# Two cross-attention layers on one core: a pair's image tokens in a shared tile, packed third blocks, merged text keys, and a Gram matrix from high halves

## The chip, the cores and the metric

The kernel runs on one core of a Trainium2 chip. The metric is the device time of one execution in microseconds (us), the median of the runs. Engines in the profile: PE is TensorE's matmul, PEld its weight load, DVE is VectorE, ACT is ScalarE, POOL is GpSimd, and SP is the queue that issues most DMAs.

## The reference

Two layers run one after the other on `x` (16 batches, 256 queries, 320 channels) with a context of 16 batches, 256 tokens, 512 channels. There are 20 heads of 16 channels.

```python
# layer 0 (the first): 77 text tokens, 179 image ("ip") tokens
q, k_t, v_t = x @ Wq, text @ Wk, text @ Wv            # split into heads
text_out = softmax(q k_t / 4) v_t                     # per head
k_ip, v_ip = ip @ Wk_ip, ip @ Wv_ip
text_probs = softmax(q . k_text / 4)                  # all channels at once, no heads
sem  = (text_probs @ text) @ ip.T / 4                 # 256 x 179 per batch
ip_probs = softmax(q k_ip / 4 + 0.5 * sem) * mask
x = (text_out + ip_probs v_ip) @ Wout + bout + x
# layer 1 (the second): 252 text tokens, 4 image tokens
probs = softmax(q k_t / 4);  text_out = probs v_t     # per head
qsem  = l2norm(probs @ text)                          # per head, 512 wide
sem   = qsem @ l2norm(ip).T
ip_probs = softmax(q k_ip / 4 + 0.5 * sem) * mask
out = (text_out + ip_probs v_ip) @ W_out + b_out + x
```

## The kernel before

**Halves.** Every matmul operand that must be precise is kept as a high half (rounded to fp32r) and a low half (the remainder). A product of two such operands takes three matmuls for each 128 rows of the contraction: high x high, high x low, low x high (`prod`, L320 to L327). A product over 512 context channels is thus 12 matmuls. `halves` (L240) makes the two: ACT casts the high half, DVE or POOL subtracts.

**Layer 0** works in slots k = 0 to 79, one for each batch and group of four heads, so ten slots for a pair of batches. In a slot (`slot0`, L911) PE does the scores of slot k+2 (`score0`, tile S, 8 matmuls), the transposed scores of slot k (`turned0`, tile T, 8 matmuls), and the product with the values of slot k-1 (`attend0`, tile P). Between them lie ACT's exponentials (L899), POOL's multiplication by the semantic factor (L902, four in a slot) and DVE's maxima (L875, L876). Keys and queries go through DRAM (`kd`, `qd`) and come back into stacks of 48 rows (`stacks0`); rows 0 to 76 of a stack hold the semantic term (casts at L843 and L846), and two further rows hold indicators, written once by four DMAs at the start (L390).

**Work for later slots** is cut into steps with due times in slots (`STEPS`); `fill` runs the steps that are due at fixed points of a slot (0.2, 0.6 and 1.0 in layer 0). PE's order is the program's order throughout; in layer 1 also the order of ACT, DVE and POOL; at the start (`begin`) SP's too. The steps of layer 0 that matter here, for a pair c with batches 2c and 2c+1:
- `k0`: load the pair's context (four DMAs of 128 channels x 512 tokens) and split it; keys of both batches: for each of two blocks of 128 channels a text product (12 matmuls of 2 x 96 columns) and an image product (12 of 2 x 180), then a third block with 64 channels for text and 64 for image (12 of 512).
- `v0`: for each batch three products of 12 matmuls with 320 columns: the first 128 tokens with the text weights, the same 128 with the image weights, the last 128 with the image weights. The first tile holds 77 text and 51 image tokens, so it is masked twice.
- `q0`: load x, split it (ACT L706, POOL or DVE L707, DVE L709 for the third block, which holds high halves in rows 0 to 63 and low halves in rows 64 to 127), and three projections of 8 matmuls with 256 columns (`project`, L717).
- `m0t`, `s0`: the semantic term. `semantic0` takes 2 x 6 matmuls of 192 columns for the text scores (L792).
- `c0`: the output projection.

**Layer 1** has slots 80 to 159, five for a batch. `both1` does scores two slots ahead and transposed scores; `norm1` (L1070) computes the norm of qsem through a Gram matrix of the text tokens, 14 matmuls of 512 columns in a slot; DVE multiplies (L1078) and POOL or DVE adds (L1080). Its steps are `k1` (keys), `o1` (queries; here the third projection block already has 5 matmuls instead of 8, `packed`), `i1`, `c1` and `t1`: `tokens1` (L660) takes two value products (12 matmuls of 320 columns) and two Gram products (12 matmuls of 256 columns each), and evacuates the Gram blocks by ACT (high) and DVE (low, L678 to L693). Between `hold` and `release` DVE operations given to `late` are kept back to the next slot.

## Time and profile before

| | |
|---|---|
| median of 3 runs | 1451.64 us |
| lowest, highest run | 1450.28, 1459.53 us |
| span of the profiled execution | 1449.8 us |
| granted TensorE clock, mean | 0.994 |
| PE / PEld / DVE / ACT / POOL busy | 97% / 80% / 81% / 65% / 79% |
| DMA moved | 215.74 MB, 149 GB/s |

The profile is of one execution on the chip; its page gives the span from the first to the last instruction and no separate time of that execution. The span lies 0.5 us under the lowest run and 1.8 us under the median. Matmuls are pipelined and overlap in the records, so what a matmul costs PE is read from the starts of consecutive groups rather than from its own duration. In rows that group instructions, the columns are line, engine, operation, output<-inputs, shapes, count, then busy us and mean ns of one, then idle time before them and what ended it. In rows of the order in time: start, length, engine, line, operation, tiles, shape, count.

### The profile page before, as it was taken

How to read it: one execution, taken by the hardware profiler on the slowest of the kernel's cores; microseconds unless marked ns; L12 is line 12 of the kernel's file. 1: busy time of each engine (PE TensorE's matmuls, PEld its weight loads, DVE VectorE, ACT ScalarE, POOL GpSimd, SP SyncE). 2: the span in 40 equal slices, each digit the busy share in tenths (PEclk: the TensorE clock that was granted, in tenths of full speed). 3: DMA queues.
4: the chain of work that ended last, by engine and by line, in shares of the span. 5: the costliest groups of instructions: out<-in, count | busy, mean ns of one | idle time of the engine just before them, and what ended most of it. 6: DMA issues, size and time to landing. Idle time of an engine off the chain costs nothing.

```text
span 1449.8 us, 35042 instructions
## 1 busy us (share of the span) xinstructions
PE 1401.7 (97%) x12166; PEld 1157.8 (80%) x12166; DVE 1174.2 (81%) x2570; ACT 937.6 (65%) x2075; POOL 1152.3 (79%) x1181
## 2 busy tenths in 40 slices
PE   7899999999999999889999999999999999999998
PEld 6788888888888888577777788878878888888865
DVE  5477777777777788867888888988998889888887
ACT  5567676767676776755666666666666666566553
POOL 4269797979787878887778887788778877887785
PEclk9999999999999999999999999999999999999999
DMA  6866575665656578575544444544454445444411
GB/s 200 197 161 181 143 186 147 163 169 155 168 151 171 145 201 232 133 188 155 158 123 124 143 141 125 154 137 140 130 150 138 139 135 149 139 136 131 130 33 50
DMA packets 236284, 215.74 MB, mean 149 GB/s; under 512 B 57834, under 2 KB 222732, under 8 KB 236108
## 3 DMA queue, kind: packets, MB, share of 16 engines
q1 hardware_dynamic: 233886, 212.53, 53.4%
q8 instruction: 97, 1.59, 0.5%
q10 hardware_dynamic: 2222, 0.98, 0.3%
q14 instruction: 79, 0.65, 0.2%
HBM read 127.32 MB, written 85.16 MB: 147 GB/s over the span
## 4 chain that ended last, share of the span: by engine, by line
PE 52%; DVE 3%; POOL 1%; issue 1%; ACT 0%; DMA 0%; ACTq 0%; DVEq 0%; POOLq 0%
PE X L1075 18%; PE X L325 9%; PE X L725 6%; PE P L1088 5%; PE T L1018 4%; PE S L1023 3%; PE P L1090 2%; PE X L1209 1%; PE X L651 1%; PE P L1055 1%; DVE mn L1024 1%; PE P L934 1%; POOL P L902 0%; DVE wt L1078 0%; POOL wt L1066 0%
## 5 line engine op out<-in xcount | busy, mean ns | idle before, releaser
L902 POOL TENSOR_TENSOR P<-P,rs 128x512 f32<-128x512 f32 x320 | 412.4, 1313 | 136.1 <-ACT P L899 136.0
L1075 PE MATMUL X<-ctb,gm 128*128 128x512 f32 x1120 | 293.3, 403 | 0.7 <-DVE wt L1078 0.7
L1066 POOL TENSOR_TENSOR wt<-P,ctb 128x512 f32<-128x512 f32 x212 | 268.1, 1293 | 0.0
L899 ACT ACTIVATE P<-T 128x512 f32<-128x512 f32 x320 | 174.7, 594 | 101.8 <-PE T L896 83.7
L1024 DVE TENSOR_REDUCE mn<-S 128x4 fp32r<-128x1008 f32 x160 | 192.1, 1200 | 58.7 <-PE S L1023 56.8
L1075 PEld LDWEIGHTS X<-ctb,gm 128*128 128x128 f32 x1120 | 202.5, 190 | 38.5 <-DVE wt L1078 0.9
L1078 DVE TENSOR_TENSOR wt<-X,wt 128x512 f32<-128x512 f32 x240 | 159.7, 682 | 4.2 <-PE X L1075 3.9
L1030 ACT ACTIVATE P<-T 128x512 f32<-128x512 f32 x212 | 115.2, 598 | 58.3 <-PE T L1018 56.6
L1080 POOL TENSOR_TENSOR wt<-wt 128x512 f32<-128x512 f32 x80 | 103.5, 1294 | 60.2 <-DVE wt L1078 60.0
L876 DVE TENSOR_REDUCE mn<-S 128x4 fp32r<-128x716 f32 x160 | 142.5, 890 | 0.0
L1065 ACT ACTIVATE ctb<-P 128x512 fp32r<-128x512 f32 x212 | 122.4, 625 | 29.4 <-PE X L1075 20.6
L934 PE MATMUL P<-P,vr 128*32 128x256 f32 x1920 | 123.7, 388 | 0.0
L725 PE MATMUL X<-ho,wF 128*128 128x256 f32 x768 | 109.0, 286 | 2.2 <-DVE ho L974 1.2
L725 PEld LDWEIGHTS X<-ho,wF 128*128 128x128 f32 x768 | 100.5, 189 | 8.8 <-DVE ho L974 2.7
L725 PE MATMUL X<-hq,wE 128*128 128x256 f32 x720 | 102.7, 286 | 4.6 <-ACT hq L706 3.3
L725 PEld LDWEIGHTS X<-hq,wE 128*128 128x128 f32 x720 | 96.4, 193 | 8.3 <-ACT hq L706 3.8
L875 DVE TENSOR_REDUCE mn<-S 128x4 fp32r<-128x308 f32 x160 | 74.8, 468 | 23.2 <-PE S L874 22.9
L945 DVE STREAM_TRANSPOSE nt<-P 128x512 f32<-128x512 f32 x80 | 57.1, 714 | 39.2 <-PE P L934 38.9
L934 PEld LDWEIGHTS P<-P,vr 128*32 128x32 f32 x1920 | 56.1, 110 | 40.8 <-issue 4.9
L874 PE MATMUL S<-ks,qs 125*128 125x256 f32 x480 | 85.7, 301 | 2.2 <-DMA ks<-kd 1.7
L874 PEld LDWEIGHTS S<-ks,qs 125*128 125x128 f32 x480 | 64.4, 189 | 28.2 <-issue 24.1
L325 PE MATMUL X<-cta,wA 128*128 128x252 f32 (+3 forms) x534 | 78.8, 292 | 7.9 <-ACT wA L244 5.7
(231 smaller groups left out, 3275.3 us busy)
## 6 DMA issues: line engine op xcount, KB each, us to landing
qd<-q SPq DMA_DIRECT2D x80, 256.0 KB
qs<-qd SPq DMA_DIRECT2D x160, 112.0 KB
ks<-kd SPq DMA_DIRECT2D x160, 112.0 KB
rawc<-in_cT_dram SPq DMA_DIRECT2D x60, 256.0 KB
kd<-kst SPq DMA_DIRECT2D x50, 256.0 KB
qs<-qd SPq DMA_DIRECT2D x60, 192.0 KB
ks<-kd SPq DMA_DIRECT2D x60, 192.0 KB
qd<-q SPq DMA_DIRECT2D x64, 128.0 KB
```

Source lines behind the costliest of these rows:

```text
L325: last = mm(out, lhs(a, k), rhs(b, k), start=i == 0, stop=i == len(terms) - 1)
L725: mm(pp, w(s, k, slice(m * 128, (m + 1) * 128)), a[:, t], start=i == 0, stop=i == len(terms) - 1)
L874: mm(sp[:, h], Q[: XROW + T0, h, t * 128 : (t + 1) * 128], K[: XROW + T0, h], start=True, stop=True)
L876: anchor(nc.vector.tensor_reduce(mn[:, 1, :, t], sp[:, :, T0:], axis=AX.X, op=ALU.max))
L899: exp = anchor(nc.scalar.activation(pt, st[p], AF.Exp, scale=SCALE))
L902: anchor(nc.gpsimd.tensor_mul(pt, pt, rs[:, t : t + 1].to_broadcast([128, 2, S])))
L934: mm(pv[32 * s : 32 * s + 32, o : o + S], v[:, vt, h : h + 32], P[k, s // 2][:, t, s % 2], start=vt < 2, stop=vt != 1,)
L1024: anchor(nc.vector.tensor_reduce(maxes[k + 2][:, :, t], sp[:, :, :T1], axis=AX.X, op=ALU.max))
L1065: nc.scalar.activation(R[k, u][:, t], P[k, u][:, t], AF.Copy, scale=0.5)
L1066: anchor(nc.gpsimd.tensor_sub(W[k, u][:, t], P[k, u][:, t], f(R[k, u][:, t])))
L1075: mm(yp, gm[:, gb], R[k, u][:, kt], start=i == 0, stop=i == len(blocks[n]) - 1)
L1078: nc.vector.tensor_mul(product, yp, w[:, n])
```

## The change

- **Layout.** A pair's context tile is now text of the first batch, image of the first, image of the second, text of the second, so that the 358 image tokens are adjacent. Each load becomes three DMAs (`Pieces`, `fetch`): at the start for four loads, later for four loads of each pair.
- **Values.** The last 51 image tokens of the first batch and the first 51 of the second share one product; five products for a pair instead of six. The shared one is evacuated in two halves of 64 partitions. There are four value tiles instead of three, and a batch's `attend0` asks for both batches' values.
- **Packed third blocks.** Layer 0's query projection is `packed`, as layer 1's was: the third block takes 5 matmuls instead of 8, with the low weights in its columns 64 to 127; its evacuation has one more DVE addition. `semantic0` has 5 matmuls for a tile instead of 6, and its key tile is loaded by four DMAs instead of two.
- **Text keys.** For pairs after the first, a text product is 4 matmuls of 312 columns (high weights times high and low context together) and 4 of 156 columns, instead of 12 of 192; DVE has one more addition. Image keys are evacuated in two pieces (51 + 51 and 128 + 128 columns).
- **Indicators** go into DRAM behind the keys (three DMAs for a pair) and come with each stack's key DMA (50 rows instead of 48). The four start DMAs, their load and cast, and eight POOL memsets of the stacks go. The cast L846 covers 1024 columns instead of 716.
- **Gram from high halves.** A Gram product is 4 matmuls of 512 columns (high x high and high x low side by side); since the norm is a symmetric form, twice high x low replaces the third term in the diagonal blocks, and one more matmul adds a transposed block. ACT has one more copy, DVE three more operations of 128 columns for a batch.
- **Image columns of layer 1.** The four image tokens' context is copied into the value weights by POOL (two small copies for a batch); the value products have 324 columns, and the two multiplications that read the Gram's last columns read those instead.
- **Query remainder.** The low half of x's third block is a subtraction on 64 partitions on POOL (DVE for the first three batches) instead of DVE's L709 on 128.
- **Due times.** Many entries of `STEPS` are changed, most by 0.2 to 1 slot.

```diff
-    "k0": (-14.4, -13.3, -13, -12.4, -12, -10.8, -10.4, -9.8, -9.4, -8.8, -8.4,),
+    "k0": (-14.4, -13.3, -13, -12.4, -12, -11.2, -10.8, -10.2, -9.4, -8.8, -8.4,),
-    "q0e": (-11.8, -11, -10, -9, -8,),
+    "q0e": (-11.8, -11, -10, -10, -8,),
-    "v0e": (-7, -5.2, -4.8,),
+    "v0e": (-7, -5, -5,),
-    "v0o": (-4, -3.8, -3.4,),
+    "v0o": (-4.4, -4.2, -3.4,),
-    "t1": (-3.2, -2.2, -2.2, -1.4, -0.2,),
+    "t1": (-3, -2.2, -2.2, -1.2, 0,),
-    "o1": (-7, -6.8, -6, -5.8, -5.4, -3.4,),
+    "o1": (-7, -6.8, -5.8, -5.6, -5.2, -3.2,),
...
+    class Pieces:
+
+        def __init__(self, src):
+            self.shape = src.shape
+            self.parts = [(slice(0, S), src[..., :S]), (slice(S, S + NI), src[..., S + T0 :]), (slice(S + NI, 2 * S), src[..., S : S + T0])]
+
+    def fetch(raw, src):
+        for at, part in src.parts if isinstance(src, Pieces) else [(None, src)]:
+            dma(raw if at is None else raw[..., at], part)
...
-    for i in range(SIZES["NR"]):
-        nc.gpsimd.memset(f(ks[i]), 0.0)
-        nc.gpsimd.memset(f(qs[i]), 0.0)
-        dma(ks[i][KS0 - 2 : KS0], ind0r.unsqueeze(1).to_broadcast([2, 4, S]))
+    indicators(0)
...
+    def text_keys(ct, ms, hi, lo):
+        n = T0 + 1
+        bk = bank()
+        kp = bk[:, : 4 * n].rearrange("p (s b t) -> p s b t", s=2, b=2)
+        for k in range(4):
+            if k:
+                mm(kp[:, 0], wk0(1, k, ms), texts(ct(0, k), n), start=False, stop=False)
+            mm(kp, wk0(0, k, ms), texts(ct(slice(None), k), n), start=k == 0, stop=k == 3)
+            if not k:
+                mm(kp[:, 0], wk0(1, k, ms), texts(ct(0, k), n), start=False, stop=False)
+        main, rest = [spread(bk, x, n + 1, T0) for x in (0, 2 * n)]
+        nc.scalar.copy(hi, main)
+        nc.vector.tensor_sub(lo, main, f(hi))
+        nc.vector.tensor_add(lo, rest, f(lo))
+
+    def image_keys(ct, w):
+        kp = bank()[:, : 2 * NI + 2]
+        prod(kp, w, lambda s, k: ct(s, k)[:, T0 - 1 : T0 + 2 * NI + 1], 4)
+        return kp[:, 1:]
...
     def keys0(c):
...
+            text_keys(ct, ms, texts(kst[:, 0]), texts(kst[:, 1]))
+            yield
+            split_images(kst[:, 0], kst[:, 1], image_keys(ct, lambda s, k: wki0(s, k, ms)))
...
     def values0_(b):
         ct, i = ct0[b // 2], b % 2
+        def product(w, at):
             vp = bank()[:, :320]
+            prod(vp, lambda s, k: ct(s, k)[:, at : at + 128], w, 4)
+            return vp
+        def put(b, t, vp, sc, p=slice(0, 128), q=slice(0, 128)):
+            V = vcols(values_of(b), V0W)
+            nc.scalar.activation(V[p, t, :, 0:16], vp[q].rearrange("p (h d) -> p h d", d=D), AF.Copy, scale=sc)
+        low, high = slice(0, 64), slice(64, 128)
+        if i:
+            vp = product(wvi0[0], S - 64)
+            put(b - 1, 1, vp, vmask[low, 2:3], high, low)
+            put(b, 1, vp, vmask[high, 3:4], low, high)
             yield
+        put(b, 0, product(wv0[0], 384 * i), masks[i][0])
+        yield
+        put(b, 2, product(wvi0[0], (T0, S + MIX)[i]), 1.0)
+        yield
+        return values_of(b)
+    def values_of(b):
+        return vr[2 * (b % 2) + b // 2 % 2]
...
     def tokens1(b):
...
+        turn = buf("turn", [128, 128], FR)
         for t, lo in ((0, 0), (1, DUP)):
+            bk = bank()
+            for k in range(4):
+                both = ct(slice(None), k)
+                mm(bk.rearrange("p (s t) -> p s t", s=2), ct(0, k)[:, lo : lo + 128], both, start=k == 0, stop=k == 3)
+                if t and k == 2:
+                    mm(bk[:, S : S + 128], turn, ident_r, start=False, stop=False)
+            g, x = bk[:, :S], bk[:, S:]
             if t == 0:
                 nc.scalar.copy(G[:, 0, :], g[:, 0:128])
                 nc.scalar.copy(G[:, 1, 4:], g[:, 128:T1])
+                nc.scalar.copy(turn, x[:, DUP:T1])
+                def first_lows(g=g, x=x):
+                    nc.vector.tensor_sub(G[:, 4, :], g[:, :128], f(G[:, 0, :]))
+                    nc.vector.scalar_tensor_tensor(
+                        G[:, 4, :], x[:, :128], 2.0, f(G[:, 4, :]), op0=ALU.mult, op1=ALU.add
+                    )
+                late(first_lows)
             else:
                 nc.scalar.activation(G[:, 2, :], g[:, 0:128], AF.Copy, scale=tm)
                 nc.scalar.activation(G[:, 3, 4:], g[:, 128:T1], AF.Copy, scale=tm)
+                def corrected(g=g, x=x):
+                    for to, high, at, own in ((G[:, 5, :], G[:, 2, :], slice(0, 128), tm), (G[:, 6, 4:], G[:, 3, 4:], slice(128, T1), tm2)):
+                        nc.vector.scalar_tensor_tensor(to, g[:, at], tm, f(high), op0=ALU.mult, op1=ALU.subtract)
+                        nc.vector.scalar_tensor_tensor(to, x[:, at], own, f(to), op0=ALU.mult, op1=ALU.add)
                 late(corrected)
             yield
...
     def split(src, eng, tag):
...
-        third = lambda: order(
-            nc.vector.scalar_tensor_tensor(hl[:, 2], f(hl[:, 2]), neg, src[:, 2], op0=ALU.mult, op1=ALU.add)
-        )
-        if clock[0] >= NS:
-            after_next(third)
-        else:
-            third()
+        order(eng.tensor_sub(hl[64:, 2], src[64:, 2], f(hl[64:, 2])))
...
     def queries(l, a, b=0):
...
+            if m == 2 and not l:
+                hi, lo = qh[:64, 0, 2], qh[64:, 0, 2]
+                nc.scalar.copy(hi, pp[:64])
+                nc.vector.tensor_sub(lo, pp[:64], f(hi))
+                nc.vector.tensor_add(lo, pp[64:], f(lo))
+                return
...
-        yield from project(l, wq[l], a, evac, l == 1)
+        yield from project(l, wq[l], a, evac, True)
...
     def semantic0(b):
...
-                for h in range(2):
+                for h in range(2 if k < 2 else 1):
...
     def stacks0(k, parts="KQTM"):
...
-                dma(K[T0 : T0 + XROW], stack_rows(kd[0][b // 2][:, :, b % 2])[:, hs])
+                rows = kd[0][b // 2].rearrange("(q h) t -> q h t", h=H)
+                dma(K[T0 : T0 + XROW + 2], rows[:, hs, S * (b % 2) :][..., :S])
...
-                    m = f(get("m0t", b)[:, 0:1, T0:]).to_broadcast([T0, 4, S - T0])
-                    order(nc.scalar.copy(K[:T0, :, T0:], m), *casts[-1:])
+                    m = f(get("m0t", b)[:, 0:1]).to_broadcast([T0, 4, S])
+                    order(nc.scalar.copy(K[:T0], m), *casts[-1:])
...
```

More of the change, by code (lines that the diff above doesn't have):

```diff
@@ L154, in xattn2 @@
     clock = [-99.0]
-    words, slots = {"ctb": 1024, "cta": 1024, "raw": 512, "rawc": 512, "kb": 576, "mt": S, "mx": 2, "kst": 4 * S, "rs": 2 * S, "P": 4 * S}, {}
+    words, slots = {"ctb": 1024, "cta": 1024, "raw": 512, "rawc": 512, "kb": 576, "mt": S, "mx": 2, "kst": 4 * S, "rs": 2 * S, "P": 4 * S, "wC": 8 * (320 + 2 * NIP)}, {}
     def buf(tag, shape, dtype=F32, bufs=1, name=None):
@@ L219, in xattn2 @@
     dma(tmask, tmask_d)
+    tm2 = const_tile([128, 1], "tm2")
+    nc.vector.tensor_scalar_mul(tm2, tmask[:, 2:3], 2.0)
     anchors = {}
@@ L452, in keys0 @@
             get("m0t", 2 * c - 1)
+            indicators(c)
             ct0[c] = yield from tiles
@@ L657, in keys1 @@
             )
+            if m == 1:
+                for k in range(2):
+                    last = ct(slice(None), slice(2 * k, 2 * k + 2))[..., T1:]
+                    nc.gpsimd.tensor_copy(w1["ip"](b % 2)[:, :, 2 * k : 2 * k + 2], f(last))
             yield
@@ L905, in attend0 @@
         b, g = divmod(k, NG)
+        get("v0", b | 1)
         v, pv = get("v0", b), bank("P")
```

257 lines of the change are left out of this document (139 added, 118 removed), and 14 rows, old and new, of the table STEPS.

## The prediction

> **What bounds the kernel now.** I read the totals first, then the busy time by stage, then PE's instructions in order of time, because the change mostly removes matmuls and all depends on whether PE's time is the program's time. The page and the windows (first totals, then 0 to 55 the start, 55 to 139 the first ten slots, then five whole pairs of layer 0, the passage to layer 1 in two pieces, the steady part of layer 1, the tail; columns: length, busy us of each engine with instruction counts, PE clock, DMA share, GB/s):
>
> ```profile
> span 1449.8 us, 35042 instructions
> PE 1401.7 (97%) x12166; PEld 1157.8 (80%) x12166; DVE 1174.2 (81%) x2570; ACT 937.6 (65%) x2075; POOL 1152.3 (79%) x1181
> 0.00:55.00 55.00, 39.77 (x244) 37.05 (x244) 25.93 (x68) 29.91 (x67) 17.80 (x37) 0.97 0.71 202
> 55.00:139.20 84.20, 80.16 (x707) 69.44 (x708) 62.76 (x141) 58.66 (x133) 62.48 (x53) 0.98 0.65 168
> 139.20:510.90 371.70, 371.55 (x3493) 321.86 (x3493) 274.17 (x661) 269.06 (x593) 315.33 (x281) 1.00 0.62 162
> 510.90:664.80 153.90, 140.53 (x1327) 115.86 (x1325) 123.48 (x276) 101.24 (x226) 127.01 (x122) 0.99 0.71 184
> 664.80:761.80 97.00, 91.31 (x749) 72.63 (x748) 80.16 (x159) 60.09 (x132) 73.49 (x75) 0.98 0.50 146
> 761.80:1377.60 615.80, 615.33 (x5183) 496.92 (x5182) 549.63 (x1138) 385.44 (x855) 504.93 (x552) 1.00 0.48 138
> 1377.60:1449.80 72.20, 63.03 (x474) 44.10 (x473) 58.11 (x130) 33.16 (x73) 51.25 (x66) 0.97 0.14 42
> ```
>
> In the two steady stages, 987 us together, PE is idle for 0.6 us, at a granted clock of 1.00. A busy PE may still be one that waits inside a pipeline, so I look whether consecutive starts are evenly spaced at what the columns cost. Layer 0, in order of time (start, length, group):
>
> ```profile
> 288.60 0.81 PE L325 MATMUL X<-cta,wA 128*128 128x192 f32 x6
> 289.25 0.83 PE L325 MATMUL X<-ctb,wA 128*128 128x192 f32 x6
> 290.01 1.50 PE L934 MATMUL P<-P,vr 128*32 128x256 f32 x24
> ...
> 294.69 1.10 PE L725 MATMUL X<-hq,wE 128*128 128x256 f32 x8
> 295.63 0.23 PE L881 MATMUL X<-ident_r,mn 128*16 128x128 f32 x1
> ...
> 309.17 1.07 PE L325 MATMUL X<-wC,cta 128*128 128x320 f32 x6
> 310.08 1.04 PE L325 MATMUL X<-wC,ctb 128*128 128x320 f32 x6
> 310.95 0.22 PE L881 MATMUL X<-ident_r,mn 128*16 128x128 f32 x1
> ...
> 315.56 1.48 PE L792 MATMUL X<-kb,q 128*128 128x192 f32 x12
> 316.88 0.22 PE L881 MATMUL X<-ident_r,mn 128*16 128x128 f32 x1
> ```
>
> From start to next start: 12 text-key matmuls of 192 columns take 1.41 us (0.1175 each), 8 projections of 256 columns 0.94 (0.1175), 12 values of 320 columns 1.78 (0.148), 12 semantic ones of 192 columns 1.32 (0.11). So a 192-column matmul costs what a 256-column one does: below some 250 columns there is a floor of about 0.11, above it the cost follows the columns. Layer 1:
>
> ```profile
> 974.66 3.44 PE L1075 MATMUL X<-ctb,gm 128*128 128x512 f32 x14
> 977.93 1.02 PE L1209 MATMUL X<-rs,rs 128*128 128x256 f32 x4
> ...
> 980.54 1.59 PE L325 MATMUL X<-cta 128*128 128x256 f32 x12
> 982.07 0.51 PE L1018 MATMUL T<-qs,ks 57*128 57x256 f32 x4
> ```
>
> 14 matmuls of 512 columns take 3.27 us, 0.234 each; the 12 of a Gram product take 1.53. The spacing leaves no hole, so in both steady stages a matmul that goes is time that goes, as long as no other engine becomes late.
>
> **What PE loses, per pair of layer 0.**
> - Values: six products become five, -1.78.
> - Packed projection: 8 matmuls become 5 in a batch's third block, 3 x 0.1175 = 0.35, for two batches -0.70.
> - Semantic: two matmuls less per batch at 0.11, for two batches -0.44.
> - Text keys: 1.41 becomes four matmuls of 312 columns and four of 156. 312 lies between 256 (0.1175) and 320 (0.148): I take 0.145. 156 columns are not in the rows; from half of that, 0.07, to the floor, 0.11 to 0.1175; I take 0.11, the row nearest to it. 4 x 0.145 + 4 x 0.11 = 1.02, so -0.39 a block (-0.36 to -0.55), two blocks -0.78.
>
> Together -3.7 us of 74.3. For **each batch of layer 1**: two Gram products of 12, at 0.12 a matmul (1.53 / 12 = 0.1275, the 256-column projections 0.1175), are 2.88; the new ones are 8 x 0.234 plus one transposing matmul at the floor of 0.11, 1.98: -0.90 (-0.84 to -1.08). The values' four columns more cost 24 x 4 columns at 0.148 / 320 = +0.05. Together -0.85 of 48.1.
>
> Where these fall: the window of five pairs holds five sets of steps, 5 x 3.7 = 18.5. A pair's steps run before its own slots, so the first ten slots hold another set, of which I count 2.7, since PE is idle there 4 of 84 us and a wait may take the place; the passage holds the last set, counted 2.0 (idle 13 of 154). The first pair's set falls into the start, where PE is busy 40 of 55 us: nothing. Thirteen Gram batches lie in the steady part of layer 1, 11.0; three before, 1.7 of 2.55. **Sum -35.9.**
>
> **What is added.** First POOL. In layer 0 it carries four multiplications a slot, and the context splits and query splits lie together in a pair's slots 6 to 9 (here 332.3 to 362.4). The new remainder is 64 x 256 on POOL, which no row has; a 128 x 256 addition is the nearest:
>
> ```profile
> 332.30:362.40 30.10, 30.10 (x287) 26.41 (x286) 21.74 (x54) 22.19 (x51) 29.10 (x26) 1.00 0.64 174
> ...
> L954 POOL TENSOR_TENSOR hsn<-tmp 128x256 f32<-128x256 f32 x16 | 12.0, 753 | 1.0 <-DVE tmp L951 1.0
> L709 DVE SCALAR_TENSOR_TENSOR hq<-hq,tmask,xq 128x256 fp32r<-128x256 f32 x32 | 28.1, 878 | 1.5 <-ACT hq L706 1.5
> L687 DVE SCALAR_TENSOR_TENSOR gm<-X,tmask,gm 128x128 fp32r<-128x128 f32 x16 | 5.6, 350 | 0.9 <-ACT gm L684 0.9
> ```
>
> POOL is busy 29.1 of 30.1 us there; two remainders of 0.75 make 30.6. With the new due times these four slots hold PE steps for about 29.3 us (four fixed parts of 3.67 and the steps' prices above). So POOL ends some 1.3 us late against PE; but PE needs a product only in the next slot, and in the other six slots POOL is idle 10 of 44 us. Taken: +1.0 for all pairs; bounds 0 and 16, if 3 us of each pair were lost.
>
> DVE in layer 1 is busy 549.6 of 615.8 us. It loses L709 (0.88, once a batch) and gains three operations like L687 (3 x 0.35): +0.2 a batch, while the batch shrinks by 0.85, so 89% becomes 91%. How close that is, in a slot's beginning:
>
> ```profile
> 984.24 0.16 DVE L1040 COPY sr<-S 128x16 f32<-128x16 f32 x1
> ...
> 984.55 0.51 PE L1023 MATMUL S<-ks,qs 56*128 56x256 f32 x4
> ```
>
> The second scores start 0.15 us after DVE's copy frees their bank: a DVE that comes into a slot more than 0.15 late holds PE, and the transposed scores behind it. The new due times put the second Gram step, with its four corrections, into the next slot, which is lighter. Taken: +1.5 (16 batches at 0.1); bounds 0 and 16 (1 us each).
>
> ACT's wider cast:
>
> ```profile
> L843 ACT CAST qs<-tph 77x1024 fp32r<-77x1024 f32 x48 | 49.8, 1039 | 0.0
> L846 ACT CAST ks<-M 77x716 fp32r<-77x716 f32 x48 | 37.7, 785 | 0.0
> ```
>
> 0.25 us in each of 64 slots, on an engine busy 269 of 372 us in that stage, ahead of the slot's exponentials; they would still meet a POOL that is the later one. Taken at nothing; with that cover gone, at most 16. The halved key evacuations, DVE's additions, key DMAs of 50 rows, and the 15 more DMAs a pair for the SP queue are hidden in the same slack.
>
> Then the **start**, where SP works through a fixed order:
>
> ```profile
> 0.73 0.39 SPq L139 DMA_DIRECT2D rawc<-in_cT_dram  x1
> 1.19 0.42 SPq L139 DMA_DIRECT2D P<-in_wk_dram  x1
> ...
> 49.01 3.74 SPq L139 DMA_DIRECT2D kd<-ho  x6
> 52.86 0.70 SPq L884 DMA_DIRECT2D qs<-mt  x1
> ...
> 54.96 0.71 PE L896 MATMUL T<-qs,ks 127*128 127x256 f32 x4 [3.13 <-DMA qs<-mt]
> ```
>
> A DMA costs SP 0.46 us. The first context becomes 12 issues instead of 4 ahead of the first keys, and the second pair's, which stands before the maxima's DMA at 52.86, too: 16 x 0.46 = 7.4 us of SP at most. Five issues for indicators go, three come; and PE has less to do before 55. I take +3.5, the middle between 0 and 7.
>
> **Sum**: -35.9 + 1.0 + 1.5 + 3.5 = -29.9, so the span goes from 1449.8 to 1419.9, and with the 1.84 us that the median (1451.64) lies above this span, **1422 us**. With every added cost at nothing and all of PE's savings (41.5: seven sets of 3.7 and sixteen of 0.85, with 2 for slack), 1408 to 1412.
>
> **The rivals.**
> - *Everything is kept* (0.15): the start is no slower, POOL and DVE keep up: 1410. For it: 0.6 us of idle in 987. Against it: the SP order at the start.
> - *POOL takes PE's place in layer 0* (0.13): four slots that now need 30.6 us of POOL wait for it, and each pair gains 0.7 instead of 3.7. Then 1422 + 16 = 1438. For it: no idle time on POOL in those slots. Against it: the lead of a slot.
> - *PE was never the limit* (0.10): DVE and POOL carry the program, both get a little more work, and the time stays, 1450. For it: busy shares of 79 to 81% beside PE's weight loads at 80%. Against it: no wait of PE in the steady stages, and starts spaced by columns alone. The Trainium skill, "Perfetto Trace Analysis", section "Identifying the Most-Contended Engine", says that a matmul's busy share is no good measure and that the share of weight loads is to be read instead; by that rule DVE, at 81%, would be the most contended engine here. The trace speaks against it: the spacing, not the share, shows PE full.
> - *DVE holds PE in layer 1* (0.06): the corrections and the delayed value multiplications bring DVE late into the slots, and the scores wait on their bank. From a mean lateness of about 0.65 us over the 80 slots (0.15 of slack, 0.5 of wait, 40 us) all is eaten; at 0.8 the time is 1422 + 52 - 1.5 = about 1472, slower than before. For it: 0.15 us of slack. Against it: L709 goes from the heaviest slot.
>
> The forecast has 0.56. **Range**: 1405, a little under "everything is kept", to 1441, over the POOL case, which leaves out the last two rivals, 0.16. A change of 1% (14.5 us) is about what a measurement here can tell from none. Faster by more than 1% (under 1437): 0.56 + 0.15 and half of the POOL case, 0.78; within 1%: the other half and "never the limit", 0.16; slower: 0.06.
>
> **What the new profile would show.** A pair in the middle of layer 0 at 70.6 us instead of 74.3 and a batch of layer 1 at 47.3 instead of 48.1, PE without idle in both; values as five groups of 12, text keys as 8 matmuls in 1.02 us, a Gram group of 4 in 0.94. If PE shows waits on POOL's L902 (new line) in slots 8 and 9, POOL's edge was reached; waits of the scores on DVE's copy show DVE's. The first transposed scores would start at about 58 instead of 55. I am wrong if the start loses more than 7 us, if the 312-column matmuls with their short rows cost more than columns, or if the passage between the layers, which waits on POOL and DMA, gets longer.

## The result and the profile after

The changed kernel takes 1446.01 us (median of 9 runs, 1441.51 to 1447.18) against 1451.64: ratio 0.994, 95% interval 0.993 to 0.996. By the ratio that is 0.6% faster (the two medians lie 5.6 us, 0.4%, apart), less than the 1% that the prediction asked of a change; 1422 was forecast, and 1446 is outside its range of 1405 to 1441. One of the prediction's own signs of being wrong is there: the start loses more than 7 us. The totals and the same seven stages as in the prediction (each boundary is the start of a slot's first transposed scores; the columns are as there):

```profile
span 1444.3 us, 34497 instructions
PE 1373.9 (95%) x11694; PEld 1117.4 (77%) x11694; DVE 1175.4 (81%) x2667; ACT 958.1 (66%) x2130; POOL 1162.9 (81%) x1237
0.00:62.70 62.70, 40.57 (x223) 37.64 (x223) 29.50 (x83) 31.17 (x71) 12.40 (x32) 0.93 0.66 181
62.70:148.30 85.60, 79.61 (x679) 68.06 (x680) 65.10 (x151) 61.43 (x140) 64.08 (x56) 0.95 0.68 174
148.30:514.50 366.20, 359.27 (x3351) 305.44 (x3350) 279.58 (x698) 279.12 (x619) 321.19 (x292) 1.00 0.63 165
514.50:668.30 153.80, 137.77 (x1270) 112.97 (x1268) 123.19 (x282) 104.41 (x228) 126.17 (x125) 0.97 0.69 186
668.30:767.00 98.70, 91.94 (x721) 70.92 (x720) 80.11 (x163) 61.30 (x134) 75.73 (x82) 0.97 0.47 139
767.00:1371.40 604.40, 602.96 (x4990) 479.50 (x4989) 540.34 (x1164) 387.93 (x868) 511.57 (x588) 1.00 0.48 140
1371.40:1444.30 72.90, 61.77 (x474) 42.87 (x473) 57.58 (x131) 32.74 (x73) 51.73 (x67) 0.99 0.14 42
```

472 matmuls are gone and PE is busy 27.8 us less, but the span is only 5.5 us shorter: PE now stands idle where it did not before. By stage, us:

| stage | before | after | change | forecast |
|---|---|---|---|---|
| start | 55.0 | 62.7 | +7.8 | +3.5 |
| slots 0 to 9 | 84.2 | 85.6 | +1.4 | -2.7 |
| five pairs, slots 10 to 59 | 371.7 | 366.2 | -5.5 | -18.5, and +1.0 for POOL |
| passage, slots 60 to 79 | 153.9 | 153.8 | -0.1 | -2.0 |
| slots 80 to 89 | 97.0 | 98.7 | +1.7 | -1.7 |
| layer 1, slots 90 to 153 | 615.8 | 604.4 | -11.4 | -11.0, and +1.5 for DVE |
| tail | 72.2 | 72.9 | +0.7 | 0 |

By stage the forecast misses some 24 us: 12.0 in the five pairs, 8.4 in the start and the first ten slots, 5.3 in the passage and slots 80 to 89, 0.7 in the tail; layer 1 gained 1.9 more than forecast.

In the steady part of layer 0 PE had no wait before. Now, in the pair of slots 40 to 49 (369.2 to 441.8, 72.6 us instead of 74.3), the view of waits has two (wait, total us, times, longest):

```profile
PE P L1048 <- POOL P L1015: 0.6, 1, 0.6
PE X L994 <- DVE mn L989: 0.5, 1, 0.5
```

The first is the attend (the product with the values, tile P) of slot 8 of the pair. In order of time, POOL's chain ahead of it and PE at that place:

```profile
413.15 5.05 POOL L1015 TENSOR_TENSOR P<-P,rs 128x512 f32<-128x512 f32 x4 [0.74 <-ACT P L1012]
418.17 2.52 POOL L284 TENSOR_TENSOR cta<-rawc,cta 128x512 fp32r<-128x512 f32 x2
420.66 0.45 POOL L1070 TENSOR_TENSOR hsn<-tmp 128x128 f32<-128x128 f32 x1
421.08 5.01 POOL L1015 TENSOR_TENSOR P<-P,rs 128x512 f32<-128x512 f32 x4
...
424.94 0.63 PE L1048 MATMUL P<-P,vr 128*32 128x256 f32 x4
426.15 1.49 PE L1048 MATMUL P<-P,vr 128*32 128x256 f32 x20 [0.58 <-POOL P L1015]
```

POOL runs without a hole from 413.15 to 426.09, and the last 20 matmuls start 0.06 us later. The second wait is slot 1's maxima: VectorE transposes, subtracts a key piece and only then reduces the scores, whose last matmul ended at 380.54:

```profile
379.94 0.72 DVE L1059 STREAM_TRANSPOSE nt<-P 128x512 f32<-128x512 f32 x1 [0.26 <-PE P L1048]
380.68 0.43 DVE L284 TENSOR_TENSOR kst<-X,kst 64x256 fp32r<-64x256 f32 x1
381.14 0.48 DVE L988 TENSOR_REDUCE mn<-S 128x4 fp32r<-128x308 f32 x1
381.54 0.89 DVE L989 TENSOR_REDUCE mn<-S 128x4 fp32r<-128x716 f32 x1
...
381.33 0.76 PE L826 MATMUL X<-hq,wE 128*128 128x256 f32 x5
382.58 0.22 PE L994 MATMUL X<-ident_r,mn 128*16 128x128 f32 x1 [0.48 <-DVE mn L989]
```

The five projection matmuls were eight before; three fewer at 0.12 us are 0.36, and a wait of 0.48 stands behind them.

At the start the maxima's DMA, last in SP's order, is issued at 60.59 instead of 52.86, behind the second pair's context (six and six DMAs, 43.26 to 54.64; four and 3.3 us before):

```profile
43.26 7.36 SPq L143 DMA_DIRECT2D rawc<-in_cT_dram  x6
51.57 3.07 SPq L143 DMA_DIRECT2D raw<-in_cT_dram  x6
54.68 1.97 SPq L143 DMA_DIRECT2D kd<-kst  x4
56.70 3.80 SPq L143 DMA_DIRECT2D kd<-ho  x6
60.59 0.73 SPq L997 DMA_DIRECT2D qs<-mt  x1
```

What SP waits for there (41 to 62 us) are above all landings of stacked loads, 4.2 and 1.9 us (2.3 and 1.8 before, 41 to 55 us). From the first of these context loads to the maxima's DMA SP takes 17.3 us for 22 DMAs, against 11.9 for 14 before:

```profile
SPq L143 <- DMA ks<-kd: 4.2, 3, 2.2
SPq L143 <- DMA qs<-qd: 1.9, 2, 0.9
```

### The profile page after: what moved, and what is told of

The parts are those of the page before. It is cut to its first block, busy times and chain, and to the rows that moved or that the text cites. A ratio compares the mean times of both kernels' runs of the same rounds, so it can differ in the third digit from the quotient of the medians.

```text
span 1444.3 us, 34497 instructions
## 1 busy us (share of the span) xinstructions
PE 1373.9 (95%) x11694; PEld 1117.4 (77%) x11694; DVE 1175.4 (81%) x2667; ACT 958.1 (66%) x2130; POOL 1162.9 (81%) x1237
## 4 chain that ended last, share of the span: by engine, by line
PE 80%; DVE 7%; DMA 4%; POOL 3%; issue 2%; ACT 2%; SPq 2%; ACTq 0%; DVEq 0%; POOLq 0%
PE X L1189 17%; PE X L364 15%; PE X L826 10%; PE P L1048 7%; PE S L986 5%; PE P L1202 5%; PE T L1132 4%; PE T L1009 4%; PE S L1137 3%; PE P L1204 2%; PE X L777 2%; SPq L143 2%; POOL wt L1180 1%; DVE mn L989 1%; PE X L1323 1%
## 5 line engine op out<-in xcount | busy, mean ns | idle before, releaser
L1015 POOL TENSOR_TENSOR P<-P,rs 128x512 f32<-128x512 f32 x320 | 407.3, 1299 | 128.0 <-ACT P L1012 127.0
L1189 PE MATMUL X<-ctb,gm 128*128 128x512 f32 x1120 | 289.1, 401 | 0.8 <-DVE wt L1192 0.8
L1048 PE MATMUL P<-P,vr 128*32 128x256 f32 x1920 | 128.4, 389 | 6.9 <-POOL P L1015 3.7
L826 PE MATMUL X<-hq,wE 128*128 128x256 f32 x672 | 97.7, 291 | 5.3 <-ACT hq L813 4.3
L826 PEld LDWEIGHTS X<-hq,wE 128*128 128x128 f32 x672 | 92.6, 198 | 10.4 <-ACT hq L813 4.8
L1132 PEld LDWEIGHTS T<-qs,ks 57*128 57x128 f32 x640 | 48.3, 185 | 49.6 <-issue 37.1
```

Of the source, the lines that this page charges most:

```text
L826: mm(pp, w(s, k, slice(m * 128, (m + 1) * 128)), a[:, t], start=i == 0, stop=i == len(terms) - 1)
L1015: anchor(nc.gpsimd.tensor_mul(pt, pt, rs[:, t : t + 1].to_broadcast([128, 2, S])))
L1048: mm(pv[32 * s : 32 * s + 32, o : o + S], v[:, vt, h : h + 32], P[k, s // 2][:, t, s % 2], start=vt < 2, stop=vt != 1,)
L1189: mm(yp, gm[:, gb], R[k, u][:, kt], start=i == 0, stop=i == len(blocks[n]) - 1)
```

## The experiments

Each edit is to the changed kernel unless it says otherwise. Slot, pair and stage lengths are differences of starts in each run's profile.

### Layer 0's pair

**Two context remainders on VectorE.**

```diff
-                halves(*ahead.pop(0), eng, wait)
+                halves(*ahead.pop(0), nc.vector if first_two and i < 3 else eng, wait)
...
```

> The changed kernel, the first two of a pair's four context remainders on VectorE instead of GpSimd from pair 2 on (1.25 us each off GpSimd in slots 6 and 7 of a pair). Theory (GpSimd is late into slot 8 since slots 6 and 7 became shorter): the attend of slot 8 waits 0.2 us or less instead of 1.0, the steady pair goes from 72.6 to 71.6 us, time 1438 to 1441. Rival (the wait only moves: VectorE's reductions or the next GpSimd products come late instead): pair 72.4 to 72.8, time 1445 to 1447.

1445.77 us. The wait in slot 8 is gone (slot 7.95 to 7.33 us) and the pairs from slot 20 on take 72.0. The time stays: slots 13 and 14 take 9.64 and 8.57 us instead of 6.51 and 6.37. The chain of what ended last, in that slot:

```profile
173.70 1.48 PE P L1049 x24
175.18 0.19 SPq L143
175.37 0.04 issue
175.42 5.21 DMA qs<-qd
180.63 0.14 issue
180.76 1.19 PE S L987 x4
```

A load of stacked queries is issued late on SP, and the scores wait for it. The wait went as the theory said, and the steady pair nearly reached its 71.6; the rival's pair of 72.4 to 72.8 did not come. The time lies in the rival's range all the same, because slots 10 to 19 lose 4.7 us. The runs below apply this edit one pair later.

**Copies ahead of subtractions.**

```diff
-            halves(spread(hi, *a, n), spread(lo, *a, n), spread(src, *b, n))
...
+        for h, l, s in parts:
+            nc.scalar.copy(h, s)
+        for h, l, s in parts:
+            nc.vector.tensor_sub(l, s, f(h))
```

> The changed kernel, where an image block of keys is split into high and low parts: both of ScalarE's copies first, then both of VectorE's subtractions, instead of copy, subtraction, copy, subtraction, which the trace shows waiting for one another in turn. Theory (VectorE's subtractions come so late in slot 1 that the reduction ahead of the maxima is late): the wait of the maxima matmul for that reduction in slot 1 falls from 0.5 us to 0.1 or less, that of slot 0 (0.7 in one pair) too, steady pair 72.6 to between 71.8 and 72.2, time 1441 to 1443. Rival (the reduction is held by the transpose of the attend's product and not by these pieces): wait and pair as they were, time 1445 to 1447.

1443.25 us, which its interval (0.992 to 0.995 of before) does not tell from the changed kernel. Slot 1 goes from 8.20 to 8.04 only; the transpose stands ahead of the reduction as before, so both sides were partly right. The pair of slots 40 to 49 goes from 72.6 to 72.5, that of slots 30 to 39 from 73.5 to 72.8.

**Both, and the third key block later.** The same two edits (VectorE from pair 3 on) and

```diff
-    "k0": (..., -9.4, -8.8, -8.4,),
+    "k0": (..., -9.4, -8.6, -8.4,),
```

> The changed kernel, start as it is, with three edits in the pair: both copies ahead of both subtractions, the first two context remainders on VectorE for pairs 3 to 7, and the third key block due 0.2 slots later (-8.6 instead of -8.8), so that its 12 matmuls stand between the scores and the maxima of slot 1. Theory (1.8 us of waits in a pair take back half of the 3.5 us of matmuls saved: slot 8's on GpSimd, slot 1's maxima on VectorE's reduction): waits of PE in the pair under 0.3 us, steady pair 70.8 to 71.4 us, time 1438 to 1441. Rival (the third block in the later place holds the next slot's attend or GpSimd instead): pair 72 or more, time 1443 to 1447.

1440.07 us, ratio to before 0.990 (0.988 to 0.992), as the theory said; the pairs are a little over its 71.4. Two take 71.5 us, two 71.9, the first, slots 10 to 19, 75.5. The view of PE's waits is empty for slots 30 to 39, whose window reads:

```profile
294.54:366.00 71.46, 71.17 (x670) 61.16 (x669) 57.96 (x141) 55.63 (x124) 62.01 (x57) 1.00 0.64 172
```

So 1.16 us of a pair's 72.62 were waits on POOL and VectorE, and 74.3 - 71.5 = 2.8 us is what a pair gains when the view lists no wait. The rows tell where the other 0.9 of the 3.7 is. Added up from each group's starts to the next group's starts, as the prediction priced them, the values, projections, semantic and text-key matmuls of slots 30 to 39 go from 22.15 us before to 18.38 here, 3.8 less. But the transposed scores take 0.65 more, the attend 0.40 and the maxima's matmuls 0.16 (the rest 0.2 less):

```profile
294.54 0.64 PE L1013 MATMUL T<-qs,ks 127*128 127x256 f32 x4
295.11 1.50 PE L1052 MATMUL P<-P,vr 128*32 128x256 f32 x24
...
297.12 0.64 PE L1013 MATMUL T<-qs,ks 127*128 127x256 f32 x4
297.60 1.15 PE L367 MATMUL X<-cta,wB 128*128 128x360 f32 x6
```

Four transposed scores take 0.57 us where the attend follows and 0.48 where keys do. Five attends of the pair now follow transposed scores directly; before, none did, and the change to the attend stood behind other groups, as behind the prediction's text keys (288.60 to 290.01). There it was priced with the group, and it stays when the group gets shorter. The attend's and the maxima's part is not traced to a cause.

**The old due times.**

```diff
-    "c0e": (5, 5.4, 6.6, 7.8, 8.6, 9.2,),
+    "c0e": (5.6, 6, 6.6, 7.2, 7.6, 8.2,),
...
```

> The changed kernel with the due times of before for the repeated steps of layer 0 (nine entries: keys, queries, values, products, semantic part and closing), the matmuls and instructions as changed. Theory (the new due times empty slots 6 and 7 of a pair, 5.9 and 7.1 us instead of 8.6 and 7.5, and GpSimd is late into slot 8): the wait of slot 8's attend is gone, the steady pair 71.8 to 72.2 us instead of 72.6, time 1441 to 1444. Rival (the new due times are what the packed and shared products need, GpSimd's lateness comes from its 1 us more of work): pair 72.8 us or more, time 1446 to 1452.

1461.63 us: the theory fell. Slot 8 takes 5.85 us (5.94 before), but slot 9 9.2, and three of four steady pairs 74.5 (the other 76.5), as before the change, although their matmuls are the new ones. In the pair of slots 40 to 49 PE waits 1.9 us:

```profile
PE P L1048 <- POOL P L1015: 0.9, 2, 0.6
PE X L994 <- ACT rs L933: 0.5, 1, 0.5
PE X L364 <- ACT P L1012: 0.3, 1, 0.3
PE X L994 <- DVE tmp L1065: 0.2, 1, 0.2
```

and in its slot 9 POOL, the last of the busy columns, works 9.06 of 9.22 us:

```profile
441.72:450.94 9.22, 8.35 (x72) 6.85 (x71) 6.40 (x21) 6.78 (x21) 9.06 (x9) 1.00 0.87 198
```

With the work where it was, the whole gain of a pair is lost, and POOL is the full engine of the slot that grew; 0.9 of the 1.9 us of waits are put down to it, the rest to ScalarE and VectorE. The new due times bring 1.9 us a pair.

### Layer 1, and the query remainder

**Layer 1's part alone**, in the kernel before: the Gram product, its values' columns and layer 1's due times; `split` as before.

> The kernel before with layer 1's part of the change alone: the Gram matrices from the high halves with a transposing matmul, the image prompt's four columns in the values' product, and layer 1's new due times; layer 0 as before. Theory (layer 1's part keeps all it was priced at, 0.85 us a batch): slots 90 to 153 from 615.8 to 603 to 605 us, layer 0 unchanged, time 1438.5 to 1441.5, below that of the whole change, so that layer 0's part costs 4 to 7 us in all. Rival (the gain of layer 1 leans on layer 0's new layout or the passage loses it): time 1444 to 1449.

1454.05 us, no gain. Two batches take 95.8 us (before 96.3, after 94.6), slots 80 to 89 101.7. In slots 113 and 114 VectorE is busy 9.19 of 10.29 and 9.54 of 10.35 us, and the third remainder is among its instructions there (0.95 us at 990.82, its median; the shortest takes 0.48):

```profile
984.84:995.13 10.29, 10.13 (x81) 7.76 (x80) 9.19 (x20) 7.18 (x19) 7.23 (x8) 1.00 0.47 121
995.13:1005.48 10.35, 10.35 (x91) 8.49 (x90) 9.54 (x22) 6.27 (x15) 10.03 (x11) 1.00 0.34 101
```

The view of waits lists none of PE's in layer 1, but the starts tell. Slots 113 and 114 are 0.34 and 0.22 us longer than in the changed kernel, at the matmuls that read what VectorE writes behind the remainder (the projections of `ho` from 992.79: one start to the next 0.35 us instead of 0.12) and at slot 114's second scores (at 997.45 and 997.64: 0.19 each to the next start instead of 0.10 and 0.11).

**The remainder back on VectorE**, all else as changed:

```diff
-        order(eng.tensor_sub(hl[64:, 2], src[64:, 2], f(hl[64:, 2])))
+        third = lambda: order(nc.vector.scalar_tensor_tensor(hl[:, 2], f(hl[:, 2]), tmask[:, 5:6], src[:, 2], op0=ALU.mult, op1=ALU.add))
...
```

> The changed kernel with the third query remainder back on VectorE in both layers (128 x 256, in layer 1 issued one unit later, as before). Theory (VectorE is at its edge in slots 3 and 4 of a layer-1 batch: the Gram corrections add 1.3 us there and only the remainder's move makes room): a pair of batches 95.6 to 95.9 us instead of 94.6, layer 1 loses 7 to 9 us; in layer 0 GpSimd's wait in slot 8 stays, since GpSimd has a gap right behind the remainder; time 1452 to 1456. Rival (the run of layer 1's part alone was slower for the old layer-0 order of work before it, not for the remainder): batches 94.6, time 1445 to 1447.

1495.32 us. Layer 1 is as expected: 95.6 to 95.8 us for two batches. Layer 0 is not: a pair takes 79 to 80 us, slot 8 of it 12.7 to 13.2. The remainder itself, 128 x 256, and what POOL does meanwhile:

```profile
460.03 4.96 DVE L816 SCALAR_TENSOR_TENSOR hq<-hq,tmask,xq 128x256 fp32r<-128x256 f32 x1
...
458.51 4.97 POOL L1021 TENSOR_TENSOR P<-P,rs 128x512 f32<-128x512 f32 x4
463.45 1.26 POOL L814 TENSOR_TENSOR hq<-xq,hq 128x512 fp32r<-128x512 f32 x1
465.40 0.46 POOL L1076 TENSOR_TENSOR hsn<-tmp 128x128 f32<-128x128 f32 x1 [0.69 <-DVE tmp L1071]
...
465.52 0.27 PE L1000 MATMUL X<-ident_r,mn 128*16 128x128 f32 x1 [4.08 <-DVE sp L912]
```

Of the 32 remainders of this kernel the shortest takes 0.48 us, the median is 0.94, and this one takes 4.96. It begins during the second of five GpSimd instructions in a row and ends at 464.99, in the first hole that POOL leaves (464.71 to 465.40); in the same place of four other pairs it takes 4.95 to 4.96 us and ends 0.3 us behind the last of the row too. The maxima matmul waits 4.08 us for VectorE. The Trainium skill, "SBUF — State Buffer", section "SBUF: two separate sides", says that VectorE with two SBUF inputs and GpSimd share a port pair under an exclusive lock, which the first holds for its whole instruction. The trace agrees that VectorE stands still while GpSimd works; here it did not get its turn between GpSimd instructions that followed one another either.

**The old Gram product**, all else as changed:

```diff
-                mm(bk.rearrange("p (s t) -> p s t", s=2), ct(0, k)[:, lo : lo + 128], both, start=k == 0, stop=k == 3)
...
+            prod(g, lambda s, k: ct(s, k)[:, lo : lo + 128], ct, 4)
```

> The changed kernel with the Gram matrices of layer 1 as before (two products of 12 matmuls, no transposing matmul, the corrections without the cross term); layer 0, the query remainder on GpSimd and the due times as changed. Theory (the Gram product is worth 0.85 us a batch where VectorE has room, and the remainder's move only makes that room): pairs of batches at 96.2 to 96.4 us as before, 94.6 with both, 95.8 with the Gram product alone; time 1456 to 1459. Rival (the remainder's move is worth 0.6 us a batch by itself): pairs of batches at 95.0 to 95.4, time 1448 to 1452.

1455.01 us (one run). Two batches take 96.0 us. So of 96.3 us layer 1's part without the remainder's move takes away 0.5 (0.7 in the run with the remainder back on VectorE), the change without the Gram product 0.3, and both 1.7: about half the gain belongs to neither part alone.

### The start and the first twenty slots

**A context piece in three DMAs, in the kernel before:**

```diff
+        cuts = (0, S, 2 * S - 77, 2 * S) if n == 2 * S and src.tensor is cT_d.tensor else (0, n)
+        for a, z in zip(cuts, cuts[1:]):
+            dma(raw[..., a:z], src[..., a:z])
...
```

> The kernel before, each piece of a pair's context loaded in three DMAs (columns 0 to 255, 256 to 434, 435 to 511) instead of one, nothing else changed. Theory (queue): the start goes from 55.0 us to 60 to 63, time 1457 to 1460. Rival 1 (issue time alone, 8 more issues for each pair, 16 before the first transposed scores of which half count): start near 58.7, time 1455. Rival 2 (matmuls and evictions of the new layout made the start late): start 55 to 56, time 1451 to 1453.

**One load a piece:**

```diff
-            src = cT_d[:, b * S : (b + n) * S]...
+            src = (cT_d, cP_d)[n - 1][:, b * S : (b + n) * S]...
...
```

> The changed kernel, with the first layer's image and text context laid out in pair order in a second input, so that each piece of a pair's context is one DMA instead of three (8 DMAs fewer for each of the 8 pairs; layer 1 reads the old layout). Theory (SP's queue lets only some eight DMAs be under way, so three DMAs for one push the later loads and the stores behind them back): the start up to the first transposed scores goes from 62.7 us back to 55 to 57, the first ten slots from 85.6 to 83 to 85, time 1436 to 1440. Rival 1 (only the 0.46 us of each issue counts: 8 fewer issues ahead of that point): start near 59, time 1442 to 1443. Rival 2 (the start is late for the matmuls and the evictions of the first pair, not for loads): start 61 or more, time 1444 to 1447.

**The first maxima on ScalarE's queue:**

```diff
-        maxima0(0, nc.sync)
+        maxima0(0)
```

> The changed kernel, the first slot's DMA of the maxima issued on ScalarE's queue, as those of all later slots, instead of on SP's behind 12 loads of context and 10 stores of keys. Theory (SP's order alone makes the first transposed scores late; the maxima's matmul is done at 52.7 us): they start at 55 to 57.5 us instead of 62.7, and the kernel keeps most of it: time 1439 to 1442. Rival (what the next slots need stands behind the same loads and stores in the queue): the start moves to 55 to 57.5, but the first ten slots grow from 85.6 us to 90 or more, time 1444 to 1447.

**Both of these:**

> The changed kernel with one DMA for each piece of a pair's context and the first maxima's DMA on ScalarE's queue; the indicator rows in three DMAs a pair, as changed. Theory (both edits shorten SP's queue, and the two long indicator DMAs of the earlier run hid it): start 53 to 56 us, start and first twenty slots together 215 to 219 us, time 1438 to 1442. Rival (several chains of the first pairs, loads, stores and the second pair's work, stand at the same edge, so that the sum does not move): together 221 to 225, time 1443.5 to 1447.

**One indicator DMA a pair** (the edit shown), **and the two edits above with two indicator DMAs for all pairs:**

```diff
-        for to, at in (...):
-            dma(rows[:, :, to], ind0_d[:, at]...)
+        dma(rows, ind0_d.unsqueeze(1).to_broadcast([2, H, 2 * S]))
...
```

> The changed kernel, a pair's indicator rows written by one DMA (the input row laid out in pair order) instead of three, so 8 DMAs in the queue instead of 24. Theory (each takes SP 0.60 us, 15 of them stand in a row from 16 to 29.6 us ahead of the first store of keys, and later ones are in the way of the first slots' loads and of ScalarE's DMA of the maxima): the start goes from 62.7 to between 59 and 61 us, the first ten slots from 85.6 to 84 to 85, time 1440 to 1443. Rival (SP has the time there, and the start is set by the pieces of context alone): start 62 to 63.5, time 1445 to 1447.

> The changed kernel with three things taken from SP's queue at the start: one DMA for each piece of a pair's context (as in the run with one load), all pairs' indicator rows in two DMAs instead of 24, and the first maxima's DMA on ScalarE's queue. Theory (the 9 us that start and first twenty slots lost come from SP's queue and its landings; one by one the loss was passed on, since the next item in the queue held the same work): start 53 to 56 us, start and first twenty slots together 213 to 217 us instead of 223.1, time 1436 to 1441. Rival (something other than the queue, the lower clock after the start's idle time or the second pair's work on VectorE and ScalarE, sets the first twenty slots): start 55 to 58, together 221 to 225, time 1444 to 1448.

**Idle matmuls:**

```diff
+        for i in range(40):
+            mm(idle[:, :S], ident_r, wkt[:, 0, 0, :S], start=True, stop=True)
         turned0(0, 0)
```

> The changed kernel with 40 matmuls of 256 columns, whose result nothing reads, put on TensorE ahead of the first transposed scores, where it waits 7 us for the DMA of the maxima (40 x 0.12 = 4.8 us at full clock, so they end before the wait does). Theory (the idle wait halves the granted clock for the 3.4 us stretches behind it): the stretches at half clock between 60 and 81 us, 5.1 us of loss in the granted clock, shrink to one at most; slots 0 and 1 go from 27.3 us to 23.5 to 25.5, the start stays at 62.7, time 1442 to 1444. Rival (slots 0 and 1 are set by VectorE, ScalarE and the queue): slots 0 and 1 at 26.5 to 28 us with the clock full, time 1445.5 to 1447.5.

| run | time | start | slots 0-9 | 10-19 | sum |
|---|---|---|---|---|---|
| before | 1451.64 | 55.0 | 84.3 | 74.6 | 213.9 |
| before, context in three DMAs | 1457.29 | 61.3 | 84.1 | 74.6 | 220.0 |
| after | 1446.01 | 62.7 | 85.6 | 74.8 | 223.1 |
| one load a piece | 1444.58 | 59.3 | 89.7 | 74.2 | 223.2 |
| first maxima on ScalarE's queue | 1446.88 | 56.3 | 88.8 | 78.7 | 223.8 |
| both of these | 1443.06 | 57.6 | 89.7 | 74.2 | 221.5 |
| one indicator DMA a pair | 1451.93 | 66.0 | 85.4 | 75.5 | 226.9 |
| both, two indicator DMAs in all | 1447.28 | 59.3 | 88.2 | 77.4 | 224.9 |
| 40 idle matmuls | 1445.43 | 62.3 | 85.1 | 74.8 | 222.2 |

(Stage lengths are of the profiled execution; with one indicator DMA a pair that was the fastest of its runs, 1447.78 us.)

In the kernel before, three DMAs for one cost 6.3 us of start: that is enough for most of the loss. Where the queue of the changed kernel is made lighter, the start comes back by up to 6.4 us, but slot 0 grows from 14.4 us to 17.6 (one load), 16.5 (maxima) and 16.1 (both), and with two indicator DMAs slots 3, 7 and 13 grow instead. In slot 0 PE then waits for the second batch's softmax (with both edits; the first line ends the start, the other two stand in slot 0):

```profile
57.61 1.19 PE L1009 MATMUL T<-qs,ks 127*128 127x256 f32 x4 [4.83 <-DMA qs<-mt]
69.47 0.34 PE L922 MATMUL X<-ident,sp 128*77 128x128 f32 x1 [0.83 <-ACT sp L918]
72.51 0.39 PE L931 MATMUL X<-tph,M 77*128 77x256 f32 x1 [2.23 <-DVE tph L925]
```

So the rival of those runs holds for the sum, 221 to 225 us: several chains stand at the same edge. One limit that they share can be read, from the first stacked loads to the maxima's DMA, before, and then with one load a piece (the last two columns are the DMA engines' busy share and GB/s):

```profile
38.30:52.90 14.60, 11.86 (x87) 11.39 (x86) 3.64 (x8) 8.58 (x16) 0.00 (x0) 1.00 1.00 243
...
40.10:57.30 17.20, 11.41 (x86) 10.94 (x84) 5.63 (x11) 10.47 (x19) 0.00 (x0) 1.00 0.93 207
```

About the same 3.55 MB takes 14.6 us in the one and 17.2 in the other with the DMA engines nearly full in both, which fits that a shorter queue did not help. Why the transfers are slower in the changed kernel stays open, and so does the last of the 9 us; merging the indicator rows made the kernel slower than the changed one (ratio to before 0.998 to 1.000), against the theory, and that too is unexplained.

The 40 matmuls took away little of the half clock: inside slots 0 and 1 it falls from 7.7 to 6.8 us, and the two slots shorten by 0.3 us. Beside the pair's edits it falls from 5.6 to 3.4 us, and they take 26.0 us instead of 25.9. So far as it was taken away, the half clock does not set these two slots; the rest is not tested.

### Put together

**Both edits of the start with two indicator DMAs in all, and the pair's first two:**

> The same, with both copies ahead of both subtractions in the image blocks' split and, from the third pair's successor on (pairs 3 to 7), the first two context remainders on VectorE. Theory (queue at the start, GpSimd in slot 8, the alternating split): steady pair 71.4 to 71.9 us instead of 72.6, time 3 to 4 us below that of the run without these two. Rival (they cost elsewhere what they gain): no difference of 2 us between the two runs.

**The pair's three, and 40 idle matmuls:**

> The run of the pair's three edits with the same 40 matmuls. Theory (pair and start add up): steady pair 71.5 us, slots 0 and 1 2 to 3 us shorter than in that run (25.9 us there), time 1437 to 1439. Rival (slots 0 and 1 are set elsewhere): as that run, 1439.5 to 1441.5.

**One load a piece, the maxima on ScalarE's queue, and the pair's three:**

> These two edits and the pair's three (both copies ahead of both subtractions, two context remainders on VectorE from pair 3 on, the third key block 0.2 slots later). Theory: the sum of both gains, steady pair 71.5 us, time 1432 to 1436. Rival: the pair's gain alone, 1438 to 1441.

1441.07, 1439.39 and 1438.60 us (ratios 0.991, 0.992 and 0.990). The first lies 6 us below its run without the pair's edits (1447.28), more than expected; beside the pair's edits alone (1440.07) none of the three shows a difference, so the start's edits add nothing: the rival. Intervals of 0.988 to 0.992 for the last and for the pair's edits alone, against 0.993 to 0.996 for the changed kernel, show both to be faster than either kernel. Of the 24 us that the forecast missed, the edits brought back some 6.

## Why the prediction was wrong, point by point

- **A matmul that goes is time that goes** (-18.5 over five pairs): 13.0 too much. The condition that it came with, "as long as no other engine becomes late", was not met. Read as they were priced, the removed groups are worth 3.8 us a pair for 3.7. For the text keys two errors cancel, which is luck: 312 columns take 0.18 us and not 0.145, 156 columns 0.08 and not the floor of 0.11, together 1.05 for 1.02. But a pair without listed waits is only 2.8 shorter, since 1.0 comes back in the groups beside them, 0.65 of it the change to the attend that the price had taken in: 4.5 us in five pairs. Waits on POOL and VectorE take 1.16 a pair: 5.8. Slots 10 to 19 and 30 to 39, 74.8 and 73.5 us, lose 3.1 more. (The sum is 0.4 over 13.0, because the first pair before took 74.6 and not 74.3.)
- **POOL, +1.0 in all** (bounds 0 to 16): this is the step that failed first. Its cover was "PE needs a product only in the next slot"; the rows show that POOL is the later one exactly there. The wait was expected in slots 8 and 9 as a sign, and stands in slot 8: 0.6 us a pair, 3 in five. The query remainder, which the prediction priced, is not what makes it: POOL idles 0.74 us right behind it, at 412.4. With the old due times a pair keeps nothing of the 3.7 us, less than the 0.7 that the rival "POOL takes PE's place" left it; POOL's waits are about half of those that the view lists there.
- **VectorE in layer 0** was taken at nothing, "hidden in the same slack". Slot 1's maxima show a wait of 0.5 us a pair.
- **The start, +3.5** (0 to 7): +7.8. The prediction counted SP's issues, 0.46 us each. The 12 context loads of the second pair took 11.4 us, not 5.5, because SP waits some 6 us among them until stacked loads that it issued earlier have landed. First ten slots, -2.7: +1.4. The two belong together: where an edit shortened the start, these slots took up to 4.1 us more.
- **Passage and slots 80 to 89, -3.7**: +1.6. PE's busy time there fell by 2.1 us (231.8 to 229.7), and waits took it. In the view of waits PE waits 5.5 us for VectorE's reduction in the passage (1.0 before), and in slots 80 to 89 the scores wait 2.5 us for VectorE's copy (1.3 before), the sign that the prediction gave for VectorE's edge. With the pair's three edits the passage takes 151.5 to 151.9 us, about what was forecast; but runs with one load a piece and without these edits come to 151.7 and 152.2, so what makes VectorE late stays open.
- **Layer 1, -11.0 + 1.5**: -11.4, batch 47.3 us as forecast. But the reason given, matmuls alone, is half of it: without the remainder's move the same matmuls bring 0.25 to 0.35 us a batch and not 0.85. The move is in the prediction only as a point against a rival, without time, so the right number is in part luck. That rival, "DVE holds PE in layer 1", has its condition met in slots 113 and 114 as soon as the remainder stays on VectorE, at a price of 0.5 to 0.6 us a batch and not 3.
- **PE was never the limit** (1450) came nearest in time and not in mechanism: take two engines' lateness away, and the time falls by 6 us.

## What to carry to other kernels

An engine without idle time is the limit only until its work shrinks: before pricing a saving in full, add up the next engine's unbroken chain from its last free moment to the instruction that needs it, slot by slot, not over four slots. Parts of a change can be worth little alone: in layer 0 the removed matmuls without the new due times brought nothing (74.5 us a pair), in layer 1 the Gram product and the remainder's move brought 0.5 and 0.3 of 1.7 us. A price read from a group's start to the next start contains the change to the group behind it, which stays. At a start, look at what DMAs move and how full their engines are before counting issues.

## What the runs showed of the hardware

- With the remainder back on VectorE, an instruction with two SBUF inputs began during the second of five GpSimd instructions in a row and ended 0.3 us behind the last, in five pairs alike (4.95 to 4.96 us for 0.48).
- Transposed scores take 0.57 us up to the attend and 0.48 up to a key product.
- The granted clock drops to half in stretches of 3.4 us (0.50 from 19.41 to 22.82 in the kernel before, 1.00 on either side), each 1.7 us of full clock. Two of them lie in the first 100 us of the kernel before (from 19.4 and 67.2) and five in the changed one (36.3 to 43.1, 60.2 to 67.0, 77.2 to 80.7). The Trainium skill, "TensorE: Matmul & The Clock Gate", section "What's actually happening", says that the clock is halved after an idle window of about 3.4 us and freed after a busy one. The length agrees; but the last PE gaps above 1 us ahead of the stretches at 19.4 and 36.3 are only 1.8 us (from 16.0) and 2.4 us (from 34.1), and the one at 67.2 in the kernel before has no gap above 0.6 us in the 12 us before it.
